# Four graph-attention layers over 4096 nodes: layer 1 with six all-node row tiles in place of eight, the two halves of a row tile multiplied together in layers 2 and 3, and layer 2's bias as three bf16 rows

## The chip, the cores and the metric

The kernel runs on one core of one Trainium2 chip. The metric is the device time of one execution in microseconds, from start to end of the program, as the median of several executions. The engines are named as the profile names them: PE (TensorE's matmuls) and PEld (its weight loads), DVE (VectorE), ACT (ScalarE), POOL (GpSimd) and SP (SyncE, which here issues transfers).

## The reference

Four layers of graph attention follow each other on x of 4096 nodes by 256 features. The 0/1 matrix adj of 4096 x 4096 has 17 entries per row in the mean, the diagonal among them. Each layer ends with a residual sum and a layer norm.

```python
def attention(s1, s2, values):                 # for each head
    e = leaky_relu(s1[:, None] + s2[None, :], 0.2)
    e = where(adj > 0, e, -inf)
    return softmax(e, axis=1) @ values

# layers 0 and 1: 4 heads of 64
Wh = x @ W[h];  s1, s2 = Wh @ a_src[h], Wh @ a_dst[h]
x = layernorm(x + concat_h attention(s1, s2, Wh))
# layer 2: 2 heads of 128, with biases
s1 = (x @ W1.T + b1) @ a1;  s2 = (x @ W2.T + b2) @ a2;  values = x @ W3.T + b3
x = layernorm(x + concat_h attention(s1, s2, values))
# layer 3: 1 head of 256, a softmax of e and one of -e
p, q = attention(+e) @ x, -attention(-e) @ x
x = layernorm(x + elu(concat(p, q) @ fc_W))
```

## The kernel before

The 4096 rows are 32 row tiles of 128. For every node and layer a projection (class `Projection`) writes a row of values and scores to memory; its steps are `transpose` (L682), `copy` (L687), `multiply` (L696 against the weights and, in the projection for layer 2 alone, L699, an fp32 matmul of `ones` [1 x 128] with the bias row `brow` [1 x 262], which adds the bias in PSUM), then `values`, `edge` and `store`. A row tile is then attended to in one of two ways.

**Sparse tiles** (class `RowTile`). While layer 0 runs, lists are built that say, for each row of a tile, which nodes it is connected to. A tile works on packed positions in two halves, `half(0)` and `half(1)`, 14 positions in all: 13 are filled by indirect gathers on POOL (L802, 6 for half 0 and 7 for half 1) and one by a plain transfer on SP (L797). ACT takes the exponentials (L912, in layer 3 L879, L880, L882), DVE masks them into `w` (L869 in layers 0 and 1, L914 in layer 2, L881 and L883 in layer 3), and PE multiplies `w` with the gathered values in `G` (L933). A half has "full" units (`FULL`: one weight tile of 128 columns) and "pairs" (`PAIRS`: two of 64 columns, for the upper and lower 64 rows): half 0 one full unit and three pairs, half 1 three full units and two pairs. An fp32 matmul shows as two records in the profile, so half a tile has 28 records in layers 2 and 3, 56 in layer 1. In layers 2 and 3 the loop at the end of `half` goes through full units and pairs for one head and then for the other: full, pairs, pairs, full in layer 2 and in half 1 of layer 3; full, pairs, full, pairs in half 0 of layer 3. Half 0's matmuls are issued in `half(0)`, half 1's in `half(1)`, one step later. The last tile of layer 3 ends with `last_half` (L988), where exponentials and matmuls go unit by unit.

The gathers' buffers `G` come from two pools, `g0` for half 0 and `g1` for half 1, with four slots each. A half takes one slot in layers 1 and 2 and two in layer 3, where the rows are wider: four tiles can be under way in layers 1 and 2, two in layer 3. `w` comes from a pool of 5, of which a half takes two in layers 0 and 1 and one in layers 2 and 3. A slot is free when the matmuls that read it are done.

**All-node ("dense") tiles**. Some row tiles are computed against all 4096 nodes with the adjacency as a mask. `WHOLE` lists them, in groups: none in layer 0, 4–7 and 28–31 in layer 1, eleven in layer 2, seven in layer 3. In layer 1 `whole_heads` takes a group of tiles together: for each of two pairs of heads, for each of 32 blocks of 128 nodes (a "unit"), SP loads the values (`vw`, L1269), DVE makes two masked weight tiles `pw` of 128 x (128 per tile of the group) (L1280), and for every tile of the group PE does one matmul at L1283 and one at L1285:

```python
for it in range(g):
    nc.tensor.matmul(bu[:, it * Wd:(it + 1) * Wd], p[up][:, it, :], ...)      # L1283
    nc.tensor.matmul(bf[:Wd, it * P:(it + 1) * P], v[:, flat * Wd:...], ...)  # L1285
```

Layers 2 and 3 do the like in `whole_rows` (L1205 to L1216).

**Order.** Layers 1 to 3 run in steps, two for each sparse tile (`half_with_whole`): transposes of projections for the next layer, the half, copies and matmuls of those projections, the finish of the tile before, and then as many dense units as `whole(step)` asks for, which spreads the layer's dense units evenly over its steps. `close` joins two layers: it finishes the last tiles and already issues half 0 of the next layer's first two tiles. `GROUPS` says after which tiles the layer norms are done together. The engines' queues are in the order in which a scheduler of the framework places these instructions, with a priority by the order of the program.

Of the kernel before, what the change touches and what calls it, by code (L numbers as in the profile page):

```python
# [37 lines left out]
F32 = mybir.dt.float32  # L38
F16 = mybir.dt.float16
BF16 = mybir.dt.bfloat16  # L40
# [5 lines left out]
ALU = mybir.AluOpType  # L46
# [4 lines left out]
P = 128  # L51
# [30 lines left out]
GROUPS = (((24, 4),), ((24, 2), (28, 1), (31, 2)), ((16, 2), (17, 1), (20, 2), (25, 1), (31, 2)), ((25, 1), (28, 3), (31, 4)))  # L82
# [7 lines left out]
HEADS = (4, 4, 2, 2)  # L90
WIDTH = (65, 65, 129, 257)
# [17 lines left out]
SLOT = max(p * r for p, r in zip(PER, ROW))  # L109
# [7 lines left out]
    (range(4, 8), range(28, 32),),  # L117
# [71 lines left out]
class Program:  # L189
# [27 lines left out]
    def weights(self, n):  # L217
# [16 lines left out]
        elif n == 2:  # L234
# [10 lines left out]
            ones = self.small.tile([1, P], F32, name="ones")  # L245
            nc.vector.memset(ones, 1.0)
            self.ones = ones
# [38 lines left out]
        return wext, brow  # L286
# [324 lines left out]
    def run(self):  # L611
        ins, nc = self.ins, self.nc
        nothing = self.small.tile([1, max(PITCH)], F32, name="nothing")
# [148 lines left out]
class RowTile:  # L762
# [3 lines left out]
    def __init__(self, layer, step, m):  # L766
        self.layer, self.step, self.m = layer, step, m
        self.slots = {}
        self.accs = None

# [69 lines left out]
    def half(self, half):  # L840
# [3 lines left out]
        if self.accs is None:  # L844
            pool = prog.ptwo[1 if n == 3 and self.step % 2 else 0]
            self.accs = [prog.bank(pool) for _ in range(2 if n == 3 else 1)]
        accs, U = self.accs, UNITS[half]
# [26 lines left out]
        if n == 3:  # L874
            if half == 1 and self.step == L.count - 1:
                return self.last_half(accs, parts, w, mh)
# [7 lines left out]
            turns = ((1,), (0,))  # L884
        else:
# [34 lines left out]
            turns = ((0,), (1,)) if n == 2 else ((0, 1), (2, 3)) if A == T else ((3, 0), (1, 2))  # L920


        for t, heads in enumerate(turns):
            for us in (FULL[half], PAIRS[half])[::-1 if t == 1 and (half == 1 or n < 3) else 1]:
                for h in heads:
                    for u in us:
                        for rows, g in parts[u]:
                            a = accs[h][rows, :Wd] if n == 3 else accs[0][rows, h * Wd:(h + 1) * Wd]
                            b = g[:, h * Wd:(h + 1) * Wd]
                            if n < 2:  # L930
                                a = accs[0][rows, h * Wd:(H + 1) * Wd].rearrange("p (s c) -> p s c", c=Wd)[:, ::H - h]
                                b = b.rearrange("p (s c) -> p s c", s=1).to_broadcast([P, 2, Wd])
                            nc.tensor.matmul(a, w[h][:, u, rows], b,  # L933
                                             start=half == 0 and u == 0 and (n == 3 or h == turns[0][0]),
                                             stop=half == 1, skip_group_check=True)
# [24 lines left out]
class Layer:  # L960
# [62 lines left out]
    def half_alone(self, m, part):  # L1023
# [11 lines left out]
        if part == 1 or self.tile(m).accs is None:  # L1035
            self.tile(m).half(part)
# [14 lines left out]
    def half_with_whole(self, m, part):  # L1051
# [12 lines left out]
        with ExitStack() as order:  # L1064
            for ins in self.last:
                order.enter_context(self.prog.tc.issue_after(ins))
            self.last = ()
            if part == 1 or self.tile(m).accs is None:
                self.tile(m).half(part)
                if self.outs:  # L1070


                    order.enter_context(self.prog.tc.issue_after(self.tile(m).exps.ins))
                    self.store_rows()
# [792 lines left out]
```

## Time and profile before

| | us |
|---|---|
| median of 3 runs | 2781.11 |
| lowest, highest | 2775.42, 2785.56 |
| the profiled execution | 2791.28 |
| its span in the profile | 2789.6 |
| layer 0, with the lists (about) | 0 to 1055 |
| layer 1 (about) | 1055 to 1765 |
| layer 2 (about) | 1765 to 2265 |
| layer 3 (about) | 2265 to 2790 |

The profiled execution is 10 us longer than the median of the others. Busy times in it are sums over one engine's instructions; engines run beside each other, so they don't add up to the span. PE's matmuls overlap each other: their start-to-start times, not their durations, are what each costs. The granted clock over the whole span is 0.835 of full speed.

### The profile page before, as it was taken

To read this page: it belongs to the slowest core of one execution; us is meant where nothing else is said; L and a number is where in the kernel's file an instruction comes from. 1 tells how busy PE (TensorE), PEld (TensorE's weight loads), DVE (VectorE), ACT (ScalarE), POOL (GpSimd) and SP (SyncE) were. 2 spreads that over 40 slices of the span, in tenths; PEclk is the share of its full clock that TensorE was granted. 3 is DMA by queue.
4 is the path that set the end of the run, shared out by engine and by line. 5 is a ranking of instruction groups with operands and counts; after the bars stand their busy time and mean duration, and the time that the engine had idled before them with its cause. 6 is when DMAs were issued, how large, how long until landed. Compare 5 with 4: busy or idle time off the path is not lost. (4 is left out here: it accounts for less than half of the span.)

```text
span 2789.6 us, 48067 instructions
## 1 busy us (share of the span) xinstructions
PE 2117.5 (76%) x15721; PEld 1687.1 (60%) x15721; DVE 1585.9 (57%) x5173; ACT 1553.1 (56%) x4852; POOL 1342.4 (48%) x1361
## 2 busy tenths in 40 slices
PE   5547767666677677688888887768888879998986
PEld 3336545455455456577777775557776757665664
DVE  3435544454454455476666775547766656666655
ACT  5446455555453455565555556446766746765663
POOL 0254533434434444644444442446556455666664
PEclk7657777777776778799989998879999989998998
DMA  8767556565543345444444443335656567778784
GB/s 276 250 199 229 157 159 179 162 171 160 164 144 91 98 141 143 117 132 125 132 126 132 128 132 112 110 99 161 162 151 174 151 191 216 231 229 253 234 244 141
DMA packets 301457, 460.55 MB, mean 165 GB/s; under 512 B 90566, under 2 KB 216107, under 8 KB 301196
## 3 DMA queue, kind: packets, MB, share of 16 engines
q0 software_dynamic: 74048, 225.87, 28.5%
q1 hardware_dynamic: 222530, 227.30, 27.4%
q10 hardware_dynamic: 4618, 4.20, 0.4%
q8 instruction: 127, 2.08, 0.3%
q14 instruction: 134, 1.10, 0.1%
HBM read 408.13 MB, written 49.08 MB: 164 GB/s over the span
## 5 line engine op out<-in xcount | busy, mean ns | idle before, releaser
L802 POOL DMA_INDIRECT G<-vals,idx x1326 | 1337.1, 1008 | 1418.9 <-issue 614.5
L933 PE MATMUL bank<-G,w 128*64 128x130 f32 (+4 forms) x8820 | 1112.9, 330 | 373.1 <-issue 340.9
L933 PEld LDWEIGHTS bank<-G,w 128*64 128x64 f32 (+1 forms) x8820 | 846.9, 173 | 614.6 <-issue 512.2
L912 ACT ACTIVATE w<-S,G 128x64 f32<-128x64 f32 (+1 forms) x3276 | 874.5, 351 | 216.5 <-PE bank L933 70.4
L1216 PE MATMUL bank<-vw,pw 128*128 128x129 f32 (+1 forms) x2304 | 399.0, 329 | 30.8 <-issue 25.8
L1216 PEld LDWEIGHTS bank<-vw,pw 128*128 128x128 f32 x2304 | 349.6, 199 | 77.0 <-issue 44.2
L869 DVE SCALAR_TENSOR_TENSOR w<-w,bank 128x1024 f32<-128x1024 f32 (+1 forms) x224 | 299.1, 1345 | 59.3 <-ACT w L912 44.1
L1280 DVE SCALAR_TENSOR_TENSOR pw<-Sw,cw,mw 128x512 f32<-128x512 f32 x256 | 184.6, 745 | 124.7 <-remote 81.4
L696 PE MATMUL bank<-wext,xT 128*128 128x268 f32 (+3 forms) x640 | 199.1, 446 | 34.3 <-ACT xT L687 20.9
L1285 PE MATMUL bank<-pw,vw 128*65 128x128 f32 x1024 | 201.0, 280 | 11.8 <-issue 11.5
L1205 ACT ACTIVATE pw<-Sw,d 128x512 f32<-128x512 f32 (+1 forms) x192 | 128.1, 678 | 134.1 <-remote 64.4
L1206 DVE SCALAR_TENSOR_TENSOR pw<-pw,mw 128x512 f32<-128x512 f32 (+1 forms) x192 | 121.8, 643 | 118.6 <-ACT pw L1205 83.9
L1283 PE MATMUL bank<-vw,pw 128*128 128x65 f32 x1024 | 176.5, 257 | 7.5 <-issue 7.3
L696 PEld LDWEIGHTS bank<-wext,xT 128*128 128x128 f32 x640 | 129.9, 220 | 66.8 <-ACT xT L687 25.0
L1283 PEld LDWEIGHTS bank<-vw,pw 128*128 128x128 f32 x1024 | 158.4, 196 | 14.6 <-issue 14.0
L879 ACT ACTIVATE w<-S,G 128x64 f32<-128x64 f32 (+1 forms) x343 | 111.6, 354 | 96.0 <-DMA G<-vals,idx 64.5
L747 ACT ACTIVATE erow<-bank,shift 4x128 f32<-4x128 f32 (+1 forms) x96 | 34.1, 355 | 202.6 <-PE bank L737 124.7
L404 ACT ACTIVATE mk<-raw 128x1024 uint8<-128x1024 int32 x128 | 129.1, 1049 | 19.8 <-DMA raw<-in_adjB_dram 13.8
L716 ACT ACTIVATE row<-bank 128x4 f32<-128x4 f32 (+1 forms) x128 | 21.4, 167 | 198.1 <-remote 74.6
L1213 DVE TENSOR_TENSOR pw<-pw,mw 128x512 f32<-128x512 f32 (+1 forms) x128 | 78.9, 621 | 78.1 <-ACT pw L1212 24.5
L687 ACT COPY xT<-bank 128x256 f32<-128x256 f32 x128 | 46.1, 363 | 128.1 <-PE bank L682 72.3
L1285 PEld LDWEIGHTS bank<-pw,vw 128*65 128x65 f32 x1024 | 106.1, 143 | 16.8 <-issue 16.7
(195 smaller groups left out, 2033.5 us busy)
## 6 DMA issues: line engine op xcount, KB each, us to landing
raw<-in_adjB_dram SPq DMA_DIRECT2D x128, 512.0 KB
G<-vals,idx POOLq DMA_INDIRECT x1326
vw<-vals SPq DMA_DIRECT2D x128, 130.0 KB
vw<-vals SPq DMA_DIRECT2D x128, 128.5 KB
S<-edge SPq DMA_DIRECT2D x56, 256.0 KB
vw<-vals SPq DMA_DIRECT2D x96, 129.0 KB
xp<-y SPq DMA_DIRECT2D x96, 128.0 KB
y<-xp SPq DMA_DIRECT2D x96, 128.0 KB
```

The costliest lines, as they stand in the source:

```text
L404: nc.scalar.activation(self.mk[:, 2 * q:2 * q + 2], src, AF.Copy)
L696: nc.tensor.matmul(pp[:, :c1 - c0], self.xT[:, k, :], wext[:, k, c0:c1], start=(k == 0), stop=(k == KT - 1 and brow is None))
L802: nc.gpsimd.indirect_dma_start(out=self.row(half, k), out_offset=None, in_=self.values[:N + 1 if half else MIX * P, :].rearrange("r (k c) ...
L869: return nc.vector.scalar_tensor_tensor(pair, pair, LEAST, mh2, op0=ALU.max, op1=ALU.mult)
L912: nc.scalar.activation(w[h][:, u, rows], S[:, h, rows], AF.Exp, bias=d(g, h))
L933: nc.tensor.matmul(a, w[h][:, u, rows], b, start=half == 0 and u == 0 and (n == 3 or h == turns[0][0]), stop=half == 1, skip_group_check=True)
L1205: nc.scalar.activation(p, S[:, h, :g], AF.Exp, bias=d)
L1206: nc.vector.scalar_tensor_tensor(p, p, LEAST, mj, op0=ALU.max, op1=ALU.mult)
L1216: nc.tensor.matmul(accs[it][:, c:c + Wd], p[:, it, :], v[:, c:c + Wd], start=(j == 0 and h == heads[0]), stop=(j == NT - 1), skip_group_ch ...
L1280: nc.vector.scalar_tensor_tensor(p[h], S[:, h], c[:, j, h:h + 1], mj, op0=ALU.max, op1=ALU.mult)
L1283: nc.tensor.matmul(bu[:, it * Wd:(it + 1) * Wd], p[up][:, it, :], v[:, up * Wd:(up + 1) * Wd], start=j == 0 and it == 0, **how)
L1285: nc.tensor.matmul(bf[:Wd, it * P:(it + 1) * P], v[:, flat * Wd:(flat + 1) * Wd], p[flat][:, it, :], start=j == 0 and it == 0, **how)
```

## The change

There are four edits. In layer 1 the all-node tiles become 5–7 and 29–31, so tiles 4 and 28 go the sparse way: 26 sparse tiles in place of 24, and two groups of three dense tiles in place of two of four. In layers 2 and 3, `half(0)` of a tile doesn't issue its matmuls (`hold`); `half(1)` issues those of both halves with `multiply_held`, in the order half 0's full unit and then its pairs, half 1's pairs and then its full units, each for both heads. The exceptions are half 0 of a layer's first two tiles, which `close` issues, and the last half of layer 3, before which what is held is multiplied. The bias for layer 2 is split into three bf16 rows, each the rounded rest of the one before (`thirds`), put in three partitions; `ones` is [3 x 128] in bf16, so L699 becomes one bf16 matmul. Lastly, the row of zeros `nothing` lies in a slot of `g1` in place of a buffer of its own.

```diff
-GROUPS = (((24, 4),), ((24, 2), (28, 1), (31, 2)), ...)
+GROUPS = (((24, 4),), ((24, 2), (29, 1), (31, 2)), ...)
 WHOLE = (
     (),
-    (range(4, 8), range(28, 32),),
+    (range(5, 8), range(29, 32),),
...
-            ones = self.small.tile([1, P], F32, name="ones")
-            nc.vector.memset(ones, 1.0)
-            self.ones = ones
+            self.ones = self.small.tile([3, P], BF16, name="ones")
+            nc.vector.memset(self.ones, 1.0)
...
-        return wext, brow
+        return wext, None if brow is None else self.thirds(brow)
+
+    def thirds(self, row):
+        nc, width = self.nc, row.shape[1]
+        out = self.small.tile([3, width], BF16, name="thirds")
+        for k in range(3):
+            one = self.small.tile([1, width], BF16, name="third")
+            nc.vector.tensor_copy(one, row)
+            nc.sync.dma_start(out=out[k:k + 1, :], in_=one)
+            if k < 2:
+                nc.vector.tensor_tensor(row, row, one, op=ALU.subtract)
+        return out
...
-        nothing = self.small.tile([1, max(PITCH)], F32, name="nothing")
+        nothing = self.g1.tile([P, SLOT], F32, name="G")[:1, :max(PITCH)]
...
-    def half(self, half):
+    def half(self, half, hold=False):
+        self.begun = True
...
             if half == 1 and self.step == L.count - 1:
-                return self.last_half(accs, parts, w, mh)
+                self.multiply_held()
+                return self.last_half(self.accs, parts, w, mh)
...
+        if n < 2:
+            for t, heads in enumerate(turns):
+                for us in (FULL[half], PAIRS[half])[::-1 if t == 1 else 1]:
+                    for h in heads:
+                        self.multiply(half, h, us, parts, w, h == turns[0][0])
+            return
+        self.held.append((half, parts, w))
+        if not hold:
+            self.multiply_held()
+
+    def multiply(self, half, h, us, parts, w, first):
...
+        for u in us:
+            for rows, g in parts[u]:
...
+                self.layer.nc.tensor.matmul(a, w[h][:, u, rows], b, start=half == 0 and u == 0 and first,
+                                            stop=half == 1, skip_group_check=True)
+
+    def multiply_held(self):
+        n, held = self.layer.n, self.held
+        heads = (0, 1) if n == 2 else (1, 0)
+        for group in (FULL, PAIRS):
+            for half, parts, w in held:
+                if half == 0:
+                    for h in heads:
+                        self.multiply(half, h, group[half], parts, w, n == 3 or h == heads[0])
+        for group in (PAIRS, FULL):
+            for half, parts, w in held:
+                if half == 1:
+                    for h in heads:
+                        self.multiply(half, h, group[half], parts, w, False)
+        self.held = []
...
-        if part == 1 or self.tile(m).accs is None:
+        if part == 1 or not self.tile(m).begun:
             self.tile(m).half(part)
...
-            if part == 1 or self.tile(m).accs is None:
-                self.tile(m).half(part)
+            if part == 1 or not self.tile(m).begun:
+                self.tile(m).half(part, hold=part == 0 and self.n > 1)
```

More of the change, by code (lines that the diff above doesn't have):

```diff
@@ L81 @@
 PAIRS = (tuple(range(1, 1 + FIRST)), tuple(range(NPAIR - FIRST)))
-GROUPS = (((24, 4),), ((24, 2), (28, 1), (31, 2)), ((16, 2), (17, 1), (20, 2), (25, 1), (31, 2)), ((25, 1), (28, 3), (31, 4)))
+GROUPS = (((24, 4),), ((24, 2), (29, 1), (31, 2)), ((16, 2), (17, 1), (20, 2), (25, 1), (31, 2)), ((25, 1), (28, 3), (31, 4)))
 LEAD = 4
@@ L769, in __init__ @@
         self.accs = None
+        self.begun = False
+        self.held = []
     def slot(self, half, s):
@@ L843, in half @@
         H, Wd, V, T, A = HEADS[n], WIDTH[n], VALS[n], TERMS[n], LOGS[n]
[L844 to L847, printed above, removed]
+        U = UNITS[half]
         parts = self.parts(half)
@@ L883, in half @@
             nc.vector.tensor_tensor(w[0], w[0], mh, op=ALU.mult)
-            turns = ((1,), (0,))
         else:
@@ L920, in half @@
             turns = ((0,), (1,)) if n == 2 else ((0, 1), (2, 3)) if A == T else ((3, 0), (1, 2))
[L923 to L935, printed above, removed]
+        if n < 2:
[4 more added lines that the diff above has]
+            return
@@ new lines, in half @@
+        self.held.append((half, parts, w))
+        if not hold:
+            self.multiply_held()
+    def multiply(self, half, h, us, parts, w, first):
+        n = self.layer.n
+        H, Wd = HEADS[n], WIDTH[n]
+        if self.accs is None:
+            pool = self.layer.prog.ptwo[1 if n == 3 and self.step % 2 else 0]
+            self.accs = [self.layer.prog.bank(pool) for _ in range(2 if n == 3 else 1)]
+        accs = self.accs
+        for u in us:
+            for rows, g in parts[u]:
+                a = accs[h][rows, :Wd] if n == 3 else accs[0][rows, h * Wd:(h + 1) * Wd]
+                b = g[:, h * Wd:(h + 1) * Wd]
+                if n < 2:
+                    a = accs[0][rows, h * Wd:(H + 1) * Wd].rearrange("p (s c) -> p s c", c=Wd)[:, ::H - h]
+                    b = b.rearrange("p (s c) -> p s c", s=1).to_broadcast([P, 2, Wd])
+                self.layer.nc.tensor.matmul(a, w[h][:, u, rows], b, start=half == 0 and u == 0 and first,
+                                            stop=half == 1, skip_group_check=True)
@@ new lines, in multiply_held @@
+    def multiply_held(self):
[11 more added lines that the diff above has]
+                        self.multiply(half, h, group[half], parts, w, False)
+        self.held = []
```

## The prediction

> **What bounds the kernel now.** I read the page's first parts, then the busy time by stretches, then the waits inside a stretch, then TensorE's timeline, where single costs can be seen. From the page:
>
> ```profile
> PE 2117.5 (76%) x15721; PEld 1687.1 (60%) x15721; DVE 1585.9 (57%) x5173; ACT 1553.1 (56%) x4852; POOL 1342.4 (48%) x1361
> PE   5547767666677677688888887768888879998986
> PEclk7657777777776778799989998879999989998998
> ...
> q8 instruction: 127, 2.08, 0.3%
> ```
>
> PE is busiest, but unevenly: 5 to 7 tenths in layer 0 (to about 1055 us) and over layer boundaries, 8 to 9 tenths inside layers 1, 2 and 3, with the clock at 0.9 there. The change works only in those last three. Busy time by stretches (the middle of layer 1, of layer 2, of layer 3, and the end):
>
> ```profile
> 1200.00:1700.00 500.00, 429.64 (x3970) 377.86 (x3970) 340.75 (x928) 285.38 (x1090) 223.07 (x221) 0.94 0.46 127
> 1850.00:2200.00 350.00, 289.09 (x2181) 250.69 (x2181) 228.99 (x798) 223.10 (x676) 211.76 (x202) 0.90 0.57 157
> 2320.00:2680.00 360.00, 328.77 (x1668) 232.04 (x1668) 230.64 (x872) 240.78 (x558) 233.74 (x229) 0.95 0.78 235
> 2680.00:2790.00 110.00, 80.93 (x420) 54.44 (x418) 62.16 (x249) 53.08 (x129) 55.94 (x56) 0.90 0.59 175
> ```
>
> The columns are PE, PEld, DVE, ACT, POOL, then the clock. The next engine is 17% to 30% behind PE. The waits in 1200–1700 say who waits for whom:
>
> ```profile
> POOL G L802 <- ACT w L912: 66.3, 10, 9.3
> DVE pw L1280 <- remote: 58.6, 25, 5.5
> PE bank L933 <- issue: 43.7, 76, 1.1
> ACT w L912 <- PE bank L933: 41.8, 18, 7.6
> ```
>
> ACT waits for PE, POOL for ACT; PE's own idle time is nearly all "issue", so no engine holds it up. I take PE as the bound in these stretches: what PE saves there is saved, until the margin of the next engine is gone.
>
> **Part 1, layer 1's dense tiles 4+4 -> 3+3.** A dense unit is 16 PE records, in groups of four (L1283 twice, L1285 twice):
>
> ```profile
> 1503.45 0.33 PE L1283 MATMUL bank<-vw,pw 128*128 128x65 f32 x2
> 1503.62 0.38 PE L1285 MATMUL bank<-pw,vw 128*65 128x128 f32 x2
> 1503.84 0.34 PE L1283 MATMUL bank<-vw,pw 128*128 128x65 f32 x2
> ```
>
> From one group to the next is 0.39 us (1503.45 to 1503.84), and each row tile has one group in a unit. A unit loses one of four groups, 0.39 us. L1283 has 858 records in 1200–1700 at 8 per unit, 107 of the layer's 128 units: 107 x 0.39 = -41.7 us. The other 21 lie at the layer's start, where PE is busy 106 of 145 us; nothing is counted for them. For two dense tiles there are two more sparse ones, four halves of 56 records. Such a half takes 4.97 us in the timeline at full clock: +19.9. A step (one half with its share of dense units) is now 13.8 us: 2034 records of L933 at 56 are 36.3 halves in 500 us. New: with what follows, (500 - 41)/40.3 = 11.4 us. The other engines' work in a step has to fit under that. The 26 new gathers leave POOL at 6.5 per step, 0.95 us each and 0.30 between: 8.1 us. ACT's busy time is 285.4/36.3 = 7.9 us. DVE's is 340.8/36.3 = 9.4 us, of which 4.2 us are L1280's 512-wide rows; these become 384 wide and fewer per step, so some 8.3 us. SP gets four transfers for each new sparse tile (scores, bits, its own row, x), of which a dense tile has scores and x already. The covers hold, DVE's as the thinnest.
>
> **Part 2, the bias.** Of L699's 64 records 44 lie in that stretch, so 22 of 32 projections:
>
> ```profile
> 1500.95 1.04 PE L696 MATMUL bank<-wext,xT 128*128 128x262 f32 x4
> 1501.93 0.70 PE L699 MATMUL bank<-brow,ones 1*128 1x262 f32 x2
> 1502.56 0.44 PE L1283 MATMUL bank<-vw,pw 128*128 128x65 f32 x2
> ```
>
> In start-to-start times, entering, between the two passes and leaving are 0.31, 0.33 and 0.31 us. That is 0.95 for what would be one ordinary step of 0.22 without a bias: 0.73 us extra. One pass goes for certain (0.33). No row shows a bf16 matmul of this shape: at worst its pass and its new operand eat up what that saves (0 saved), at best it runs in no time (0.53). L1283's two records (65 columns, 0.17 us from 1503.45 to 1503.62) are the nearest row to so short a pass: I take 0.43 saved. 22 x 0.43 = -9.5, and -2 for the ten others, which lie where PE waits more. Setting up the three rows is three casts, two subtractions and three small DMAs, each later cast waiting for the DMA before it (estimated at 2 us, by ACT's longest wait for a gather in layer 3, 2.2 us). They are issued at the boundary of layers 0 and 1; DVE's last rows of layer 0 stand behind the waiting cast, and PE's first work of layer 1 behind those: +2 (0 to 4). On SP the three DMAs stand ahead of loads of vw, whose pool holds six, so that PE has up to six units' values in hand: nothing; without that lead they would cost the same 2 us again.
>
> At the clock granted in the stretch (0.94) the PE terms are (-41.7 + 19.9 - 9.5 - 2)/0.94 = -35.
>
> **Instruction loading.** About once per 16 KB of PE's instructions (q8 has 127 packets of 16.4 KB for all engines) PE issues one matmul per 0.7 to 1.4 us for a while, though nothing that it needs is late:
>
> ```profile
> 1507.69 3.21 PE L933 MATMUL bank<-G,w 128*128 128x130 f32 x47
> 1511.90 0.45 PE L933 MATMUL bank<-G,w 128*64 128x130 f32 x4 [0.99 <-issue]
> 1513.33 0.99 PE L933 MATMUL bank<-G,w 128*64 128x130 f32 x4 [0.98 <-issue]
> 1514.77 0.37 PE L933 MATMUL bank<-G,w 128*128 128x130 f32 x1 [0.44 <-issue]
> ```
>
> I find 64 us in such places in 1200–1700, over 33 blocks: 2 us each. The change takes 1024 PE instructions out of the dense units, adds 448 and saves 64 in the bias: 640 fewer, 2.5 blocks of 256, -5 us. The Trainium skill ("Runtime: NRT & Kernel Launch", section "Instruction fetch mechanics") says that the sequencer fetches the next 16 KiB block of 256 instructions while it works on the last, mostly hidden. By the rule this term is 0; I go by the rows.
>
> **Part 3, a row tile's matmuls in one go.** PE's weight-load rows in layer 3 show what a change between 128- and 64-column weights costs:
>
> ```profile
> 2440.40 0.41 PEld L933 LDWEIGHTS bank<-G,w 128*128 128x128 f32 x2
> 2441.14 1.06 PEld L933 LDWEIGHTS bank<-G,w 128*64 128x64 f32 x12 [0.33 <-issue]
> 2442.59 0.30 PEld L933 LDWEIGHTS bank<-G,w 128*128 128x128 f32 x2 [0.39 <-issue]
> 2443.22 1.06 PEld L933 LDWEIGHTS bank<-G,w 128*64 128x64 f32 x12 [0.33 <-issue]
> ```
>
> At each change the loads stop for 0.33 to 0.39 us; in matmul starts it is 0.31 against 0.217 us without a change, and the next matmul is late too: 0.15 us per change. A layer-3 tile has six changes now, two after; a layer-2 tile four and two. 25 tiles x 4 x 0.15 = 15 us; 21 x 2 x 0.15 = 6. Of these the shares inside the stretches that PE fills (360 of about 525 us, 350 of 500) are -10 and -4: -14. The matmuls are neither more nor fewer.
>
> The price: half 0's gathers lie in their slots until half 1 is multiplied, about 4.5 us longer (half a step's dense work lies between them). In layer 3 gathers of tile m wait for tile m-2's slots; the gathers of a tile take 13 x 1.25 = 16.3 of a 19.4 us tile period, and ACT is 5.5 to 20 us ahead of PE, so slack shrinks from some 15 to 8 us but holds. At the end no later tile covers it: +3 (0 to 6).
>
> A rule speaks against holding. In the middle of layer 3 PE is granted 0.95 of its clock, because the dense units (24 records, 5.4 us) fill the gaps between tiles. The skill ("TensorE: Matmul & The Clock Gate", section "HAM oscillation — how this bites in real kernels") warns that a wait of over about 3.4 us throws the clock to half until PE has been busy again as long. If held matmuls left one such gap per tile, 46 tiles would lose up to 1.7 us each: +78 by the rule. I take 0, since the dense units remain between the blocks; how many the planner leaves for the last tiles is the doubt.
>
> **Sum**: -35 - 5 + 2 - 14 + 3 = -49. I cut it to -46, because some of the 64 us of slow places may not shrink. Profiled run 2791.3 (span 2789.6) -> about 2745; the median of the three runs shown, 2781.1, is 10 us below it: 2735.
>
> **Rivals.**
> *Slower: a sparse step in layer 1 costs its chain, not PE's sum.* A step goes gather, exponential, mask, matmul, slot free; POOL's 66.3 us behind ACT and ACT's 41.8 us behind PE could be this loop. If the step stays at 13.8 us while there are 52 in place of 48, layer 1 gains 4 x 13.8 = +55, the bias saves nothing, and with +2 and -11 it is +46: 2827. It decides from a mean step of 12.6 us (508 us over 40.3 steps); at 13.2 the time is about 2805. Against it: PE is not seen waiting for ACT or DVE. Chance 0.16.
> *The hold gains nothing.* The layer-3 slots come free too late and gathers set the pace: +1 us a tile over 18 tiles eats the -14 and a little more: 2748 to 2770. For it: POOL waits 32.4 us for L933 in 2320–2680. Chance 0.22.
> *Layer 1 gives half*: the slack goes to ACT and POOL, now 8 us of an 11.4 us step: 2757 to 2785. Chance 0.16.
> *More comes free*: fewer blocks and changes also end stalls in layer 2 and before 1200: 2700 to 2715. Chance 0.08.
> *That the change doesn't do what it says* can't be: the instruction order has the two halves' matmuls together, and 38,053 in place of 38,414 rows on PE; the dense units have three groups.
>
> **The numbers.** The forecast as summed has a chance of 0.38 and spans 2715 to 2755. About 0.3% (8.3 us) is what a measurement of this kernel can tell from no change. Faster: 0.38 + 0.22 + 0.08 + 0.09 of layer 1's half = 0.77; same is the rest of that and the mildest 0.01 of the slower rival, 0.08; slower 0.15. The range 2704 to 2782 leaves out the slower rival and the deep end of the last.
>
> **What would show it.** Right: mean step of layer 1 11 to 12 us, L1283 768 records, L699 half as many; layer 3's loads stopping twice per tile; the clock still over 0.93 in layer 3. Wrong: PE waiting for ACT w L912 or DMA G in layer 1 (the slower rival), POOL waiting for L933 over 60 us in layer 3 (the hold), or the PE clock below 0.9 there.

## The result, and the profile after

The change makes the kernel slower on the chip of the first comparison: 2913.76 us (four runs, 2893.89 to 2918.80) against 2781.26 us, ratio 1.0465 with a 95% interval of 1.0410 to 1.0519. The forecast was 2735. On another chip, where the kernel before takes 2018.20 us, the same pair gave 2009.97 us, ratio 0.9951 (0.9930 to 0.9972): 0.5% faster. Most of what follows is about what lies between these two results.

Where the time went on the first chip. A layer is counted in the trace from its first dense matmul on PE to that of the next layer (layer 0 from the start). The last column is the prediction's sum of -49 by layers:

| us | before | after | forecast |
|---|---|---|---|
| layer 0, with the lists | 1097 | 1092 | +2 |
| layer 1 | 667 | 677 | -40 |
| layer 2 | 485 | 568 | -4 |
| layer 3 | 540 | 571 | -7 |

From the page of the changed kernel:

```profile
span 2907.8 us, 47608 instructions
...
PE 2117.4 (73%) x15397; PEld 1708.4 (59%) x15397; DVE 1551.5 (53%) x5213; ACT 1572.3 (54%) x4964; POOL 1361.3 (47%) x1387
...
PE   5546766667577675888788876666756789887886
...
PEclk7657777767767787888988988778877889989997
...
q8 instruction: 124, 2.03, 0.3%
```

PE does 324 matmul records fewer than before and is busy just as long (2117.4 against 2117.5 us): a record takes longer in the mean. The dip to 5 to 7 tenths about two thirds of the way, with the clock at 7 and 8, is layer 2. The stretches that answer to those shown of before (middle of layer 1, layer 2, middle of layer 3, end; PE, PEld, DVE, ACT, POOL, then the clock):

```profile
1200.00:1700.00 500.00, 404.80 (x3567) 349.60 (x3564) 306.56 (x898) 301.23 (x1171) 242.83 (x244) 0.89 0.48 134
1850.00:2280.00 430.00, 299.61 (x2238) 269.57 (x2237) 233.92 (x819) 229.24 (x685) 214.02 (x205) 0.80 0.47 129
2400.00:2780.00 380.00, 327.94 (x1639) 245.30 (x1638) 225.95 (x877) 234.83 (x550) 229.45 (x227) 0.93 0.75 221
2780.00:2907.00 127.00, 94.16 (x465) 67.68 (x463) 63.85 (x258) 56.70 (x143) 61.07 (x62) 0.84 0.58 168
```

In layer 1 PE starts 3567 records in 500 us where it started 3970, with 0.89 of its clock in place of 0.94. In layer 2 about as many records (2238 and 2181) take 430 us in place of 350. The waits of layer 2 after the change:

```profile
ACT pw L1243 <- remote: 96.6, 25, 10.3
POOL G L815 <- ACT w L923: 91.9, 9, 17.0
DVE pw L1244 <- ACT pw L1243: 91.7, 38, 6.7
PE bank L707 <- ACT xT L698: 49.7, 6, 11.4
```

and of before, over 350 us of the same layer:

```profile
DVE pw L1206 <- ACT pw L1205: 48.7, 38, 3.8
ACT pw L1205 <- remote: 36.0, 20, 3.6
POOL G L802 <- ACT w L912: 35.0, 12, 6.3
```

All of them wait longer, and in long single waits (7 to 17 us). "Remote" stands for a semaphore whose giver the view can't name. What one of these waits is, PE's timeline of the changed kernel shows:

```profile
2003.28 0.27 PE L748 MATMUL bank<-ident,row 128*1 128x128 f32 x1
2003.39 0.38 PE L693 MATMUL bank<-ident,y 128*128 128x128 f32 x2
2003.61 0.61 PE L1254 MATMUL bank<-vw,pw 128*128 128x129 f32 x4
2005.16 0.39 PE L1254 MATMUL bank<-vw,pw 128*128 128x129 f32 x2 [0.94 <-issue]
2016.01 3.56 PE L707 MATMUL bank<-wext,xT 128*128 128x256 f32 x8 [10.47 <-ACT xT L698]
```

PE seems to wait 10.5 us for ACT's copy. But the copy waits for the transposes at 2003.39, and ACT is held too: its timeline has one `pw` at 2004.47, the next at 2009.48 and 2014.45.

```profile
2004.47 0.72 ACT L1243 ACTIVATE pw<-Sw,d 128x512 f32<-128x512 f32 x1 [2.03 <-PE bank L693]
2009.48 0.72 ACT L1243 ACTIVATE pw<-Sw,d 128x512 f32<-128x512 f32 x1 [3.80 <-remote]
2014.45 0.72 ACT L1243 ACTIVATE pw<-Sw,d 128x512 f32<-128x512 f32 x1 [4.01 <-remote]
```

The semaphore that ACT waits for there is PE's own. In the trace's semaphore updates PE's count rises at 2004.45, 2009.45 and 2014.43, then three times by 2015.27, although all matmuls ahead of the multiply had been started by 2005.3. So the completion of PE's work came late, by up to 10 us, and the wait for ACT only hands this back to PE. Over 1765 to 2340 us, 64 of PE's updates come more than 1 us after the end of the last matmul recorded, 39 of them more than 3 us; in layer 2 of before about 30 and one. None of ACT's or DVE's updates in those 575 us comes over 0.3 us late. Both kinds of place, this and the one matmul per 0.7 us that the prediction took for instruction loading, are called slow stretches from here on: gaps of over 0.45 us between the starts of PE's matmuls, joined where at most 3 us lie between two of them, from the first gap's start to the last one's end, if that is more than 1.5 us.

They come with the gathers. POOL just then:

```profile
1996.47 0.94 POOL L815 DMA_INDIRECT G<-vals,idx  x1 [13.34 <-ACT w L923]
1997.72 1.14 POOL L815 DMA_INDIRECT G<-vals,idx  x1 [0.30 <-issue]
1999.16 1.14 POOL L815 DMA_INDIRECT G<-vals,idx  x1 [0.30 <-issue]
2000.60 0.95 POOL L815 DMA_INDIRECT G<-vals,idx  x1 [0.30 <-issue]
...
2012.05 0.95 POOL L815 DMA_INDIRECT G<-vals,idx  x1 [0.30 <-issue]
```

After 13 us without work POOL issues a tile's 13 gathers in a row, 1996 to 2013, and PE's slow stretch is 2004 to 2016.5. Counting PE's matmul starts against the place of a gather in its run: in layer 1 of before about 10 per us during the second to fourth gather, 6.3 at the fifth, 3.1 at the sixth, 2.4 at the seventh; in layer 2 after the change 8.9 at the fourth, 2.7 at the seventh, and 0.6 to 1.7 from the eighth to the thirteenth. Apart from a layer's start, the gathers go in runs of 6 and 7 in layers 1 and 2 of before, and the median stretch is 3.6 us in layer 1 and 5.2 in layer 2; in layer 2 after the change they go in runs of 13, and the median stretch is 12 us. Stretches make 224 us of layer 2 in place of 161, which is 63 of the 83 us lost there. Holding makes the runs so: a tile's half 0 and half 1 give back their slots at the same moment. In layer 3, where a gather's rows are wider, the fall comes later: there PE keeps its 4 to 5 starts per us up to the tenth gather and is at 0.9 to 2.5 from the eleventh to the thirteenth (after), and 10 of the runs of before were of 13 already, 19 after; stretches make 149 us of that layer in place of 114.

### The profile page after: what moved, and what is told of

The parts are those of the page before. It is cut to its first block, busy times and chain, and to the rows that moved or that the text cites. A ratio compares the mean times of both kernels' runs of the same rounds, so it can differ in the third digit from the quotient of the medians.

```text
span 2907.8 us, 47608 instructions
## 1 busy us (share of the span) xinstructions
PE 2117.4 (73%) x15397; PEld 1708.4 (59%) x15397; DVE 1551.5 (53%) x5213; ACT 1572.3 (54%) x4964; POOL 1361.3 (47%) x1387
## 4 chain that ended last, share of the span: by engine, by line
PE 53%; issue 15%; another core or an unknown queue 5%; ACT 5%; DMA 2%; DVE 1%; POOL 1%; SPq 0%; POOLq 0%; ACTq 0%; DVEq 0%
PE bank L956 28%; PE bank L1254 11%; PE bank L707 4%; ACT w L923 3%; PE bank L1323 3%; PE bank L1321 2%; DMA G<-vals,idx 1%; PE bank L693 1%; POOL G L815 1%; PE bank L538 1%; PE bank L540 1%; DVE w L880 0%; PE bank L520 0%; PE bank L748 0%
## 5 line engine op out<-in xcount | busy, mean ns | idle before, releaser
L815 POOL DMA_INDIRECT G<-vals,idx x1352 | 1356.0, 1003 | 1516.7 <-issue 625.4
L956 PE MATMUL bank<-G,w 128*64 128x130 f32 (+5 forms) x9044 | 1157.6, 339 | 403.4 <-issue 364.1
L956 PEld LDWEIGHTS bank<-G,w 128*64 128x64 f32 (+1 forms) x9044 | 904.8, 178 | 638.7 <-issue 533.4
L923 ACT ACTIVATE w<-S,G 128x64 f32<-128x64 f32 (+1 forms) x3388 | 897.1, 350 | 111.4 <-remote 50.0
L1254 PEld LDWEIGHTS bank<-vw,pw 128*128 128x128 f32 x2304 | 358.1, 201 | 134.0 <-issue 97.5
L707 PE MATMUL bank<-wext,xT 128*128 128x268 f32 (+3 forms) x640 | 207.3, 462 | 102.3 <-ACT xT L698 68.7
L1243 ACT ACTIVATE pw<-Sw,d 128x512 f32<-128x512 f32 (+1 forms) x192 | 127.8, 679 | 190.5 <-remote 137.3
L1318 DVE SCALAR_TENSOR_TENSOR pw<-Sw,cw,mw 128x384 f32<-128x384 f32 x256 | 150.9, 613 | 74.8 <-PE bank L1321 40.6
L891 ACT ACTIVATE w<-S,G 128x64 f32<-128x64 f32 (+1 forms) x343 | 109.0, 354 | 107.4 <-DMA G<-vals,idx 64.3
L1323 PE MATMUL bank<-pw,vw 128*65 128x128 f32 x768 | 153.5, 289 | 4.1 <-issue 4.1
L1321 PE MATMUL bank<-vw,pw 128*128 128x65 f32 x768 | 136.4, 266 | 7.2 <-issue 7.2
L729 DVE COPY row<-bank 128x6 f32<-128x6 f32 (+3 forms) x128 | 20.3, 159 | 209.5 <-ACT row L727 182.2
L1321 PEld LDWEIGHTS bank<-vw,pw 128*128 128x128 f32 x768 | 123.9, 206 | 10.6 <-issue 8.2
L1246 ACT ACTIVATE pw<-Sw,d 128x512 f32<-128x512 f32 (+1 forms) x128 | 83.0, 657 | 66.7 <-remote 39.6
```

Of the source, the lines that this page charges most:

```text
L707: nc.tensor.matmul(pp[:, :c1 - c0], self.xT[:, k, :], wext[:, k, c0:c1], start=(k == 0), stop=(k == KT - 1 and brow is None))
L815: nc.gpsimd.indirect_dma_start(out=self.row(half, k), out_offset=None, in_=self.values[:N + 1 if half else MIX * P, :].rearrange("r (k c) ...
L923: nc.scalar.activation(w[h][:, u, rows], S[:, h, rows], AF.Exp, bias=d(g, h))
L956: self.layer.nc.tensor.matmul(a, w[h][:, u, rows], b, start=half == 0 and u == 0 and first, stop=half == 1, skip_group_check=True)
L1243: nc.scalar.activation(p, S[:, h, :g], AF.Exp, bias=d)
L1254: nc.tensor.matmul(accs[it][:, c:c + Wd], p[:, it, :], v[:, c:c + Wd], start=(j == 0 and h == heads[0]), stop=(j == NT - 1), skip_group_ch ...
```

## The experiments

The times of the kernel before differ between chips, so each ratio is to runs of that kernel on the same chip, taken with it. A layer's length from a single trace is less certain than a ratio: layer 0, which most edits leave alone, took 1073 to 1106 us in the traces of the third chip. Theory A: gathers from POOL slow PE from about the sixth in a row on, until some 2 us after the last, and the change makes more of them (layer 1) and longer runs of them (layers 2 and 3).

**The parts alone** (second chip; before 2731.06 us).

```diff
-    (range(4, 8), range(28, 32),),     # swap: this and its GROUPS entry, in the kernel before
+    (range(5, 8), range(29, 32),),
```

> Edit: the kernel before with layer 1's all-node tiles 5-7, 29-31 alone (26 sparse tiles); bias, matmul order and holding as before. In the trace of the changed kernel layer 1 ends 13 us later than before, not 38 earlier. Theory A (each burst of 6 or 7 gathers on POOL slows PE to one matmul per 0.7 us for some 3 us, so each of the four more sparse halves costs its matmuls and such a stretch, and the lower clock the rest): +10 to +25 us, 2791 to 2806. Rival B (layer 1's loss comes from the bias split, whose set-up or whose matmul is dear): the swap alone gains as forecast, about -30, 2750.

Measured: 2760.77 us, ratio 1.013 (1.0068 to 1.0193), +35 us by the ratio. Layer 1 took 668 us; in the run below, whose layer 1 is that of before, 641. Slow stretches in it: 197 us in 40 against 155 in 36. PE's clock from 1200 to 1600 us is 0.91 against 0.96. Theory A's range was a little too low; rival B falls. The 27 us are one pair of traces, though. Over the traces of all three chips with the slow-down (those that leave its gathers as they were), layer 1 took 641 to 687 us in five kernels with groups of four and 655 to 679 in six with groups of three, with 155 to 188 us of slow stretches against 193 to 215: what the swap saves on PE is used up by stretches, and whether layer 1 ends longer or shorter is within the scatter.

```diff
+                self.tile(m).half(part, hold=part == 0 and self.n > 1)   # hold: with multiply_held, in the kernel before
```

> Edit: the kernel before with the matmuls of a row tile in one go in layers 2 and 3 alone; layer 1 and the bias as before. Both theories of the hold expect the loss seen in the changed kernel's trace in layers 2 and 3 (79 and 31 us): +90 to +115, 2871 to 2896. If holding were harmless and the loss came from layer 1's swap setting layers 2 and 3 off differently, it would be -10 to +10.

Measured: 2827.63 us, ratio 1.035 (1.0310 to 1.0391), +96 us, inside the expected range. Layer 2 took 555 us and layer 3 551.

```diff
-                self.tile(m).half(part, hold=part == 0 and self.n > 1)   # nohold: in the changed kernel
+                self.tile(m).half(part, hold=False)
```

> Edit: the changed kernel without holding: each half's matmuls are issued in its own step, in the new order (half 0 full units then pairs, half 1 pairs then full units, both heads together); swap and bias split stay. Theory A: bursts of 6 and 7 as before in layer 2, so layers 2 and 3 come back to their length before or shorter by the saved changes of weight width (4 to 10 us), layer 1 keeps its +13: 2780 to 2800. If the loss lay in the new order of the matmuls and not in the holding: 2880 or more.

Measured: 2747.48 us, ratio 1.006 (1.0027 to 1.0094). Layer 1 666, layer 2 471, layer 3 532 us. Against `hold` on the same chip, not holding saves 84 us in layer 2 and 19 in layer 3. Slow stretches make 143 us of layer 2 in place of 219. Layer 2 with holding (`hold`), then without (`nohold`):

```profile
1740.00:2250.00 510.00, 348.65 (x2609) 309.94 (x2608) 272.95 (x936) 274.71 (x810) 248.20 (x245) 0.79 0.46 127
```

```profile
1760.00:2200.00 440.00, 352.02 (x2733) 306.51 (x2732) 288.01 (x1002) 281.40 (x835) 263.35 (x249) 0.90 0.56 153
```

So the loss there lies in holding and not in the new order.

**Is it the run of gathers or the exposed wait?** (second chip)

```diff
+                if prog.gathered is not None and n in (2,) and half == 1 and k == 0:      # after_gap
+                    for _ in range(3):
+                        with prog.tc.issue_after(prog.gathered.ins):
+                            prog.gathered = nc.gpsimd.memset(self.slot(half, (k + PER[n] - 1) // PER[n]), 0.0)
```

> Edit: the changed kernel, with three POOL memsets of half 1's gather slot before half 1's gathers in layer 2, so that a tile's 13 gathers go as 6, a pause, and 7. Theory A (held tiles free both halves' slots at once, their 13 gathers go in one burst, and from about the seventh on PE issues only one matmul per 0.7 to 1.4 us until some 2 us after the last): the slow stretch of layer 2 shrinks from about 12 us per tile to two of about 3, layer 2 gets back 50 to 75 of its 79 us: 2840 to 2865. Rival C (with half 0's matmuls gone from between a projection's transpose and its multiply, PE waits for ACT's copy of xT): the pause changes nothing in that order, 2905 to 2920, and PE's wait for xT stays at about 70 us.

Measured: 2814.68 us, ratio 1.0314 (1.0263 to 1.0365). Layer 2 took 482 us, 73 less than with holding alone on this chip. The waits of layer 2 with holding and without the pauses (`hold`, over 430 us), then with them (over 380 us):

```profile
ACT pw L1244 <- remote: 121.4, 36, 6.1
PEld bank L708 <- ACT xT L699: 57.7, 8, 12.0
```

```profile
ACT pw L1251 <- remote: 32.1, 12, 4.1
PEld bank L708 <- ACT xT L699: 30.9, 8, 11.5
```

ACT's wait for PE's late semaphore falls from 121 to 32 us although PE's order is the same. The pause doesn't split every run: of 28 in layer 2, 18 are of 6 or 7 and 10 of 13 (half 1's seven gathers and the next tile's six without a pause), where 16 of the 18 of `hold` were of 13. Slow stretches make 155 us in place of 219, the longest still 17 us. Layer 3, which the edit doesn't touch, took 590 us in this run; that isn't explained. With it, the whole kernel got back only about 1.5% (1.0465 to 1.0314, on two chips), some 42 us, less than expected.

Later, on a third chip (before 2801.43 us), the other side of the question:

```diff
+        early = part == 0 and self.n == 2        # a_cover2: dense units ahead of the projection's multiply
+        if early:
+            self.whole(2 * m + part)
         for proj in projs:
             proj.multiply()
```

> Edit: the changed kernel; in layer 2's steps that hold half 0, the step's dense units come ahead of the projection's multiply, so that 16 to 24 dense matmuls (in place of 3 to 5) lie between the transposes and the multiply that waits for ACT's copy. Rival C: PE's wait for xT (50 us in layer 2) goes and layer 2 gets back 50 to 80 us. Theory A: the wait for xT becomes slow single matmuls elsewhere, layer 2 gets back 0 to 20 us.

Measured: 2925.96 us, ratio 1.0394 (1.0321 to 1.0467), layer 2 572 us (568 in the changed kernel on the first chip). The wait for the copy is nearly gone in the groups of the page, but the dense matmuls now start late instead:

```profile
L707 PE MATMUL bank<-wext,xT 128*128 128x268 f32 (+3 forms) x640 | 197.4, 442 | 27.1 <-ACT xT L698 16.3
```

```profile
PE bank L1259 <- issue: 72.2, 91, 10.8
```

The group had 102.3 us of idle time in the changed kernel. Covering the wait moved it. Rival C falls.

**Pauses between gathers in the kernel before** (third chip, before 2788.88 us). One edit with three settings: memsets of the row about to be gathered, on POOL.

```diff
+                if prog.gathered is not None and n in (1,) and k == 4:     # b_pause1: ten; b_spread1: at every k, two;
+                    for _ in range(10):                                      # b_spread0: in layer 0, at every k, three
+                        with prog.tc.issue_after(prog.gathered.ins):
+                            prog.gathered = nc.gpsimd.memset(self.row(half, k), 0.0)
```

> Edit: the kernel before, with two short POOL memsets of the destination row ahead of every gather of layer 1, so that its gathers come every 1.8 us or so in place of every 1.25. Theory A (PE is slowed by gathers that follow each other without a pause, from the sixth on): the slow stretches of layer 1 shrink or go (188 us in 39 of them in the trace of before, 155 in 36 in the layer-1 part of the run that only holds), layer 1 is 20 to 80 us shorter, PE starts per us stay near 10 at the sixth and seventh gather. Rival D (the prediction's reading: the stretches belong to the loading of PE's instruction blocks): nothing changes in them, 0 to +15 us.

> Edit: the kernel before, with ten short POOL memsets (about 3 us) ahead of the gather with k = 4 in every half of layer 1, so that a half's gathers go as 3 or 4, a pause, and 3. Theory A in the form that the number of gathers in a row counts: slow stretches gone or nearly, layer 1 20 to 80 us shorter. If it is the time since the burst's start that counts, or the last gathers whatever comes before: stretches stay at some 3 us per half, 0 to +15. Rival D: 0 to +15.

> Edit: the kernel before, with three short POOL memsets ahead of every gather of layer 0, where the 13 gathers of a tile come in one burst every 30 us and PE starts about one matmul per us from the seventh on (562 us in slow stretches, though PE isn't the only bound there). Theory A: slow stretches fall by half or more, layer 0 is 30 to 150 us shorter. Rival D: slow stretches stay, 0 to +20.

Measured: b_spread1 2752.50 us, ratio 0.984 (0.9802 to 0.9878); b_pause1 2745.75, 0.9805 (0.9760 to 0.9851); b_spread0 2868.05, 1.0271 (1.0234 to 1.0308). Layer 1 was 661 and 648 us in the first two, and 664 to 687 in three runs of this chip that leave its gathers alone (b_spread0, order_bias, b_ref), so the trace of layer 1 explains only part of the 45 to 54 us (its own 16 to 39 in b_pause1). Nor did the stretches go. With the gathers spread, about 2.05 us apart all through the layer, there are still 163 us in 26, the longest 14 us, but for one at the layer's end: against theory A, a gap between single gathers doesn't protect PE. With the pause there are 149 us in 32; it fell between one half's first gathers and the rest of it, so that runs of 6 and 7 remained. In layer 0 POOL's own time grew and took the layer from 1102 (b_ref) to 1188 us, with 612 us of slow stretches in place of 571, where theory A had expected half. So what it is in a series of gathers that slows PE, their number in a row, their pace or a backlog, stays open. The kernel gains from the pauses in layer 1 on this chip; these runs don't show by what.

```diff
-                self.tile(m).half(part, hold=part == 0 and self.n > 1)   # order_bias: in the changed kernel,
+                self.tile(m).half(part, hold=False)                      # with WHOLE and GROUPS as before too
```

> Edit: the changed kernel without holding and with layer 1's all-node tiles 4-7, 28-31 as before: what is left is the bias split and the new order of each half's matmuls. From the runs without holding (1.006 of before) and with the swap alone (1.013): -15 to -25 us. By the prediction's terms: -9 for the bias, -4 to -8 for the order. If both are nothing: 0.

Measured: 2797.48 us, ratio 1.0008 (0.9978 to 1.0037): nothing, where 15 to 25 us were expected, or 13 to 17 by the prediction's terms.

**Gathers away** (third chip). The test that decides:

```diff
             pos = half * HALF + k - 1
+            if n == 2:                        # a_plain2: the changed kernel; b_plain1: the kernel before, n == 1
+                nc.sync.dma_start(out=self.row(half, k), in_=self.values[m * P:(m + 1) * P, :ROW[n]])
+                continue
```

> Edit: the changed kernel, with layer 2's 13 indirect gathers per tile replaced by 13 plain transfers of the same size on SP (each takes the tile's own 128 rows, so the lookup of neighbours is left out of layer 2, the rest is as it was). Theory A (indirect gathers from POOL slow PE): the slow stretches of layer 2 (224 us in the changed kernel's trace) nearly vanish and layer 2 is 80 to 150 us shorter than in the changed kernel, in spite of holding. Rival C (holding exposes PE to ACT's copy of xT): layer 2 stays within 20 us of its 555 to 568.

> Edit: the kernel before, with layer 1's 13 indirect gathers per tile replaced by 13 plain transfers of the same size on SP (the tile's own rows; the lookup is left out of layer 1). Theory A: the slow stretches of layer 1 (about one of 3 to 4 us per half) nearly vanish: 60 to 150 us faster. Rival D (they belong to PE's instruction blocks): they stay, 0 to +20.

Measured: b_plain1 2586.95 us, ratio 0.9221 (0.9165 to 0.9277); a_plain2 2660.56 us, ratio 0.9503 (0.9434 to 0.9572). Both gains are larger than theory A had expected. Stretches of the middle of layer 1, first with gathers (the kernel before on this chip, `b_ref`), then without (b_plain1), then layer 2 of the changed kernel without (a_plain2):

```profile
1200.00:1700.00 500.00, 425.98 (x3790) 377.27 (x3790) 330.14 (x869) 267.87 (x1027) 219.27 (x222) 0.91 0.45 125
```

```profile
1200.00:1450.00 250.00, 250.00 (x2648) 230.78 (x2648) 230.80 (x644) 183.00 (x711) 0.00 (x0) 1.00 0.62 175
```

```profile
1900.00:2050.00 150.00, 148.87 (x1361) 140.26 (x1361) 133.87 (x516) 135.48 (x432) 0.00 (x0) 1.00 0.78 223
```

With the same bytes moved by plain transfers (460.5 MB in each trace) PE is never idle in the middle of layer 1, has its full clock and starts 10.6 records per us in place of 7.6, at a higher DMA share. Layer 1 takes 491 us in place of 687 and has 28 us of slow stretches in place of 188, all in its last 50 us, where layer 2's gathers begin; layer 2 takes 327 us in place of 572 (a_cover2, this chip) and has 3 in place of 240. Neither the bytes nor the DMA engines' load slow PE, then, but the indirect gathers that POOL issues. The edit changes the issuing engine, the queue and the rows that are read all at once; which of these counts, no run separates. Rival D falls as well: b_plain1 has all of the instruction blocks,

```profile
q8 instruction: 127, 2.08, 0.3%
```

as many as before, and no stretches but at the layer's end. There remains a rival in between: that gathers delay the loading of PE's instructions. The trace of before speaks against it: of the 39 stretches in its layer 1, 9 overlap a packet of q8 and 3 one of q14 (the other instruction queue), and q8's packets take 0.96 us in the median outside the stretches and 0.99 inside.

> No edit: the kernel before, for a trace on the chip of these runs. Layers as in its first trace within 2%.

Measured: 2812.67 us, one run. Layers 1102, 687, 484 and 539 us, layer 1 3% longer than in the first trace.

**A chip without the slow-down.** The last six kernels ran on two chips on which the kernel before takes 2018.49 and 2018.20 us.

```diff
+                if prog.gathered is not None and n in (2,) and half == 0 and k == 1:    # b_merge2, in the kernel before
+                    for _ in range(1):
+                        with prog.tc.issue_after(prog.gathered.ins):
+                            prog.gathered = nc.gpsimd.memset(self.row(1, 0), 0.0)
```

> Edit: the kernel before, with one short POOL memset of half 1's gather slot ahead of half 0's gathers of each tile in layer 2: POOL waits there until half 1's slot is free, so that a tile's 13 gathers go in one burst, while PE's order, the matmuls and the holding stay as before. Theory A: slow stretches of layer 2 lengthen to about 10 us per tile, layer 2 is 40 to 85 us longer than its 484: +40 to +85. Rival E: the burst's length is harmless, 0 to +15.

> Edit: the changed kernel, with layer 1's 13 gathers per tile replaced by plain transfers of the tile's own rows on SP (the lookup left out in layer 1). In the kernel before with the same edit layer 1 took 491 us. If the prediction's sum for PE is right once the gathers are away (-42 to -50 dense, +20 sparse, -9 to -12 bias): 450 to 465 us. If the sum itself was wrong (a dense tile saves less, a half costs more than 5 us of PE): 480 or more.

> Edit: the kernel before, with layer 2's gathers replaced by plain transfers of the tile's own rows on SP. In the changed kernel with the same edit layer 2 took 327 us. Theory A (holding costs only through the gathers): 325 to 340, holding is then worth 0 to 8 us. Rival E (holding has a price of its own on PE): under 310.

> Edit: the kernel before, with POOL memsets ahead of the gather with k = 4 of every half, ten in layer 1 (3.8 us, as in the run that gave 0.98 of before) and five in layer 2 (1.9 us). If pauses on POOL help layer 2 as they helped layer 1: 2700 to 2745 where before is 2790; if POOL's time becomes the bound in layer 2: 2750 to 2790.

Measured: b_merge2 2028.91 us, ratio 1.0053 (1.0035 to 1.0071); a_plain1 (the edit of b_plain1 in the changed kernel) 1996.13, 0.9872 (0.9837 to 0.9907), layer 1 425 us; b_plain2 (that of a_plain2 in the kernel before) 1967.33, 0.9733 (0.9708 to 0.9758), layer 2 331 us; b_pause12 (b_pause1, with five memsets in layer 2 as well) 2218.12, 1.0973 (1.0945 to 1.1002). On this chip gathers leave PE alone. Here is layer 1 of the kernel before, gathers and all (from b_plain2, which changes only layer 2):

```profile
800.00:1100.00 300.00, 300.00 (x3180) 277.22 (x3181) 277.08 (x752) 221.20 (x853) 204.41 (x196) 1.00 0.65 180
```

PE is never idle and has 1.00 of its clock, as without gathers on the third chip; POOL's gathers are as fast as ever (0.95 us, 0.30 between). Layer 1 takes 477 us, layer 0 679. In the changed kernel (after_again) the 333 gathers of layer 1 follow each other without one pause of over 0.6 us, and there are 16 us of slow stretches in the layer. In the traces of b_merge2 and after_again no update of PE's semaphore comes over 0.3 us late, but for the last two or three of the program. So b_merge2 can't tell what it was made for: whether a run of 13 costs time by itself where gathers do slow PE was tried only by its opposite, after_gap. And pauses that gained 2% on one chip lose 10% on another, where POOL has no time to give away. Two more results: a_plain1's layer 1 came out below the range that its expectation gave for a right sum (425 us, 450 to 465 expected), so the sum was not too large for PE; and without gathers layer 2 takes 331 us without holding and 327 (third chip) with it, so holding has no price of its own on PE, and that rival falls.

> No edit: the changed kernel. On a chip where gathers leave PE alone: layer 1 about 440 us in place of 477, holding worth -10 to +20, so 1985 to 2010 where before is 2018. On a chip with the slowdown: about 1.045 of before again.

> Edit: the changed kernel without holding (swap, bias split and the new order of the matmuls stay). On a chip where gathers leave PE alone: 1965 to 1985 where before is 2018 if holding costs time there too, 1990 or more if holding gains. On a chip with the slowdown: about 1.006 of before again.

Measured: the changed kernel 2009.97 us, ratio 0.9951 (0.9930 to 0.9972); without holding 1988.93, ratio 0.985 (0.9808 to 0.9891). Layers 1, 2, 3 with holding: 444, 399, 487 us; without: 442, 392, 473. The middle of layer 3, with holding and without:

```profile
1560.00:1960.00 400.00, 370.20 (x2073) 286.25 (x2070) 269.56 (x1045) 288.56 (x687) 294.59 (x289) 0.97 0.84 263
```

```profile
1550.00:1950.00 400.00, 383.89 (x2136) 288.35 (x2134) 281.47 (x1063) 296.74 (x702) 307.13 (x300) 0.99 0.86 271
```

and in the waits ACT's wait for half 0's own row, which SP loads into the slot that is held:

```profile
ACT w L891 <- DMA G<-vals: 44.1, 14, 6.9
```

```profile
ACT w L891 <- DMA G<-vals: 11.4, 9, 2.3
```

Holding costs 21 us here, 7 in layer 2 and 14 in layer 3. The waits point to slots that come back late, so that ACT waits for what is loaded into them: a loss of the kind that the second rival of the prediction described. No version was found that beats both kernels on every chip: without holding, the changed kernel is at 0.985 and 1.006; b_pause1 is at 0.9805 (0.9760 to 0.9851), but it was run only with the slow-down, and b_pause12, which has its pauses and more, lost 10% without it.

## Why the prediction was wrong, point by point

**What bounds the kernel.** The step "PE's own idle time is nearly all 'issue', so no engine holds it up" failed. PE was the busiest engine, but part of its time was neither work nor a wait that the view names: gathers were slowing it. In layer 1 this was 687 - 491 = 196 us, more than any term of the sum. The second step that failed, and the dearer one, is the price of holding: +3 in the sum, +103 measured with the slow-down (part 3). A smaller slip: the next engine lay 17% to 24% of a stretch behind PE, not up to 30%; nothing hangs on it.

**Instruction loading.** The step that gave the stretches of one matmul per 0.7 us to instruction blocks failed. Gaps came about as often as blocks, probably because a step of layer 1 has about as many PE instructions as a block: 3970 matmuls and as many weight loads over 36.3 steps are 219, against 256. With gathers away they go, and the blocks stay. They were also larger than the 64 us counted in 1200–1700: 113 us from start to end by the definition above. The Trainium skill's sentence in "Runtime: NRT & Kernel Launch", section "Instruction fetch mechanics", that fetching is mostly hidden, is in agreement with b_plain1: 127 blocks, PE busy 250.00 of 250 us. The rule was right to weigh zero; the row was read wrongly.

**Part 1.** The sum for PE was about right. On the chips without the slow-down layer 1 went from 477 to 444 and, without holding, 442 us: -33 and -35, where the sum gave -33 at full clock without its block term. In part this is luck, since errors cancel: a sparse half was priced at 4.97 us, a row's length from its first start to its last end; start to start the clean halves take 3.91 us (half 0) and 4.80 (half 1), in before too, so four cost 17.4 and not 19.9, while nothing was counted at the layer's ends. The term that failed with the slow-down is that a sparse half costs PE its matmuls alone: in layer 1 of before the median half took 7.0 us, and the added halves brought stretches that used up the gain. The mean step came out at 13.2 us (2116 records of L956 in 500 us), where 11.4 was forecast. Of the 49 us of the sum, 40 were to be gained in this layer, whose limit wasn't the one named.

**Part 2.** Right in size on PE: from the last product to the next matmul 0.949 us before, 0.528 after, 0.42 saved, where 0.43 was forecast. In the whole kernel the bias and the new order gave nothing on a chip with the slow-down (order_bias). The cost of the set-up doesn't show: layer 0 was 5 us shorter, well within its scatter.

**Part 3.** The saving was right: at full clock the two clean halves of a layer-3 tile take 4.06 + 4.68 = 8.74 us before and 8.15 held, of a layer-2 tile 2.11 + 2.57 = 4.68 and 4.34: 0.59 and 0.35 saved, where 0.60 and 0.30 were forecast. The new order alone, without holding, saves 0.44 and 0.20 of it (8.30 and 4.49 in nohold_again), so much of the gain could be had without the price. The price was wrong. It was put at a slack that shrinks "from some 15 to 8 us but holds", with +3 at the end. The runs showed +84 in layer 2 and +19 in layer 3 (hold against nohold) with the slow-down, and +7 and +14 without it. What was looked at was whether the slots come back in time; what was missed is that both halves' slots come back together, so that 6 and 7 gathers become 13. The signs named for this didn't come: POOL waited 18.6 us for L956 in the middle of layer 3, where over 60 was to be the sign.

**The clock.** The Trainium skill's rule in "TensorE: Matmul & The Clock Gate", section "HAM oscillation — how this bites in real kernels", was set to 0. In layer 3, where it was feared, the clock stayed at 0.93 (0.95 before). In layer 2 it fell from 0.90 to 0.80 with stretches of 10 us and more, and rose to 1.00 without gathers. Before, in and at the end of the stretch shown above:

```profile
1996.30:2003.00 6.70, 6.70 (x56) 6.31 (x53) 5.53 (x22) 4.79 (x19) 5.11 (x5) 1.00 0.60 145
2004.00:2013.00 9.00, 0.61 (x4) 0.40 (x3) 2.59 (x8) 2.16 (x5) 6.86 (x8) 0.78 0.54 157
2013.00:2016.50 3.50, 0.49 (x1) 0.49 (x2) 1.29 (x2) 2.05 (x6) 0.00 (x0) 0.50 0.29 58
```

PE was held up while its clock was still full, so the clock was not the cause; but after some 9 us nearly without work it was at half, as the rule has it (that the half clock then lasts as long again stands in the same page's section "What's actually happening"). How much of layer 2's loss is the clock's, no run separates; 20 of the 83 us lie outside the slow stretches.

**The rivals.** The slower rival, that a step of layer 1 costs its chain, had the side right and the mechanism wrong: layer 1 grew by 10 us, not 55, and the greater loss was in layers 2 and 3 (83 and 31 us). "The hold gains nothing" had the mechanism that remains on a chip without the slow-down.

## What to carry to other kernels

Idle time put down to "issue", and matmuls that start at a steady odd pace, are not free PE time: line them up against what every other engine does in the same microseconds before giving them a cause, and take the suspected neighbour away once to see what it costs. A change that frees several buffers at the same moment also bunches the transfers that wait for them; ask how long a run of them gets, not only whether it starts in time. And where the traces show an engine slowed from outside, measure on a second chip before trusting the sign of a change of a few per cent.

## What the runs showed of the hardware

The same program takes 2018 us on two chips and 2731 to 2801 us on others. In the trace the difference is that on the slower ones, in layers 1 and 2, PE falls from about 10 matmul starts per us to 2 or 3 at the sixth and seventh gather in a row, and to about one beyond it, until 1 to 2.5 us (median) after the last gather, with its semaphores up to 10 us late in the runs of 13; POOL's gathers themselves keep the same pace on both. Replacing the gathers by plain transfers of the same bytes makes layer 1 of a slower chip (491 us) nearly as fast as that of the others (477 us). Gathers are shown as the cause in layers 1 and 2 alone. Of the some 770 us between the two kinds of chip about 420 lie in layer 0 (1097 and 679 us), and no run took its gathers out. Why some chips do this, and whether it is the chip or its state at that time, stays open.
